# A fused RWKV and mixture-of-experts layer on one core: four PSUM places for the head's transposes, k weights loaded earlier, more products in the head

## The chip, the cores and the metric

The kernel runs on one core of one Trainium2 chip. The metric is the device time of one execution in microseconds; the time before is the median of three runs. A core has five engines that take their instructions in order, each from its own queue: TensorE (PE, matmuls; its weight loads are shown as PEld), VectorE (DVE), ScalarE (ACT), GpSimd (POOL) and SyncE (SP, which here only issues DMAs). Matmuls write to PSUM; all else lies in SBUF or in DRAM.

## What is computed

The input x has 2048 rows (tokens) of 512 float32 values. The reference normalises each row and adds to x the results of two branches that both read the normalised rows:

```python
xn = _layernorm(x, axis=-1)
# branch 1: RWKV attention; x is (1, 2048, 512): one sequence of 2048 tokens
r, v, k = jnp.split(einsum('btc,dc->btd', xn, W_rvk), 3, axis=-1)
def step(carry, kv):                  # p, q, o per channel
    no = maximum(o, u + kt);   A = exp(o - no);      Bc = exp(u + kt - no)
    y = (A * p + Bc * vt) / (A * q + Bc)
    no2 = maximum(w + o, kt);  A2 = exp(w + o - no2); B2 = exp(kt - no2)
    return (A2 * p + B2 * vt, A2 * q + B2, no2), y
attn = einsum('btc,dc->btd', sigmoid(r) * y, W_out)
# branch 2: 8 experts and 4 "zero" experts, the best 2 of 12 per token
probs = softmax(xn @ classifier_w.T)
_, idx = top_k(probs + bias, 2);  rw = take_along_axis(probs, idx) * 1.5
expert_out = (silu(xn @ gate.T) * (xn @ up.T)) @ down.T        # per expert, 256 wide
ffn = sum over chosen experts of rw * expert_out + xn * (weight of the chosen zero experts)
out = x + attn + ffn
```

The step over time runs in order over the tokens, per channel.

## The kernel before

**Sizes and units.** The 2048 rows are four blocks (b = 0 to 3) of 512 rows; each block is four tiles of 128 rows. The 512 channels are four groups (c) of 128. A *unit* is one (b, c): 512 tokens of 128 channels. `units` lists the 16 of them, b slowest. For each unit `project(b, c)` (L259) makes three products k, v and r, in this order, each a sum over four matmuls into one PSUM place `mm` (two of them), then a copy to SBUF by ACT (for r an Exp). `project` is a generator that yields after each matmul; a float32 matmul appears in the trace as two records. This document calls one such yield a *step*: a unit has 12, a product (or group) 4. `fill(n)` (L340) emits n steps of the generator `products`, which covers the first LEAD = 4 units.

**Order.** The order of the instructions is written out by hand (`manual_schedule`): each engine gets its instructions in the order in which the Python program emits them. There are three stretches.

1. *The head* (L347 to L356). SP first issues the loads in the order of L107 to L123: x block 0, the classifier `cls`, x block 1, the k weights (`load_w(2)`), x blocks 2 and 3, the v weights (`load_w(1)`), the r weights (`load_w(0)`), small vectors, `w_out`. A load of a block of x is four DMAs of 256 KB, a `load_w` is one DMA of 1 MB. Then, per block: `norm` (mean and variance on DVE, the root `sd` on ACT, some small DVE operations, then x normalised in place, two row tiles on DVE and two on ACT, and stored to DRAM as `xs`); `turn_block` (16 PE transposes, four into each PSUM place `pt` of pool `ps_tr`, each place copied by ACT to `xnT`); `logits` (PE into `lg`, also of `ps_tr`, copied by ACT to `lgs`) and `add_quarters` (PE into `pl`). The loop emits them in this order:

```python
norm(0)
turn_block(0)
for b in range(NTB):
    if b + 1 < NTB:
        norm(b + 1)
    logits(b)
    fill(1)
    if b + 1 < NTB:
        turn_block(b + 1)
    add_quarters(b)
```

2. *Routing* (L359 to L548). DVE chooses the best two of 12 for all tokens, PE counts and sorts them into 25 tiles of 128 (token, expert) pairs (`pc`, then two sums of 16 matmuls into `pi`, which wait for DVE's `tok`), and the results are the tile's tokens and weights. Steps of products are put between by `fill(9)`, `fill(14)`, `fill(7)`. Then come the first gathers and weights of experts, the first scan (unit 0), `fill(2)`, `fill(4)`, `fill(4)`, and what is left of the first four units.

3. *The loop* (L774 to L812). A table of planned times is filled and sorted: for each unit the scan's four stages (`scan`, L282: DVE scans, ACT Exps, the reciprocal; UNIT = 19 apart), the products of the other 12 units and eight output tiles of `attention` as 44 groups of four steps, and for each of the 25 tiles `first_half` (L669: loads for tile i + 2, the up and gate matmuls `pg`, tanh, gather for i + 3) and `second_half` (L685: `unite(i + 1)` makes `xgT`, `flip(i + 2)` starts a DMA transpose, `finish(i - 2)` makes the down product `po`, `yo` and a scatter that adds to `out`). The work is emitted in the order of the planned times; the times themselves are not used by the chip. Then the output tiles of blocks 2 and 3 follow, the last ones on rows read back from `out`.

**Buffers.** A pool with n buffers gives a tile one of n places per tag in turn, and a write into a place waits until the readers of its last content are done. `ps_tr`, `ps_gu`, `ps_o` and `ps_mm` have two PSUM places each; `ps_gu` (tag `gu`) is used by the experts' `pg` alone. `kvp` has four places for each of k, v and r. `ex_p` has two and `wk1` one.

Of the kernel before, what the change touches and what calls it, by code (L numbers as in the profile page):

```python
# [26 lines left out]
F32 = mybir.dt.float32  # L27
# [8 lines left out]
P = 128  # L36
T = 2048
C = 512
CC = C // P
# [20 lines left out]
def layer(ctx: ExitStack, tc: tile.TileContext, x, w_rvk, w_out, decay, first, cls, ebias, gu, down, out):  # L60
    nc = tc.nc

    def pool(name, bufs, **kw):
        return ctx.enter_context(tc.tile_pool(name=name, bufs=bufs, **kw))
# [8 lines left out]
    basep = pool("base", 4)  # L73
    rp = pool("route", 1)
    small = pool("small", 2)
    kvp = pool("kv", 4)
    wk = pool("wk", 2)
    ex_p = pool("exp", 2)
    dram = pool("dram", 1, space=bass.MemoryType.DRAM)
# [10 lines left out]
    def load_x(b):  # L90

        if b < 3:
            t = ewp.tile([P, NJ, C], F32, tag="gw", name=f"x{b}")
        else:
            t = xyp.tile([P, NJ, C], F32, tag="xy", name=f"x{b}")
        for j in range(NJ):
            i = b * NJ + j
            nc.sync.dma_start(t[:, j, :], x[i * P : (i + 1) * P, :])
            xt[i] = t[:, j, :]
# [3 lines left out]
    def load_w(n):  # L103
        wrvk_sb[n] = keep.tile([P, CC, C], F32, tag=f"wrvk{n}", name=f"wrvk{n}")
        nc.sync.dma_start(wrvk_sb[n], w_rvk[n])

    load_x(0)  # L107
    cls_sb = const.tile([P, CC, QW], F32, tag="cls", name="cls_sb")
    nc.sync.dma_start(cls_sb, cls)
    load_x(1)  # L110
    load_w(2)
    load_x(2)
    load_x(3)
    load_w(1)
# [80 lines left out]
    def norm(b):  # L195
        js = slice(b * NJ, (b + 1) * NJ)
        for j in range(NJ):
            i = b * NJ + j
            st = small.tile([P, 6], F32, tag="st", name=f"st{i}")
            nc.vector.bn_stats(st, xt[i])  # L200
            nc.vector.bn_aggr(mv[:, i, :], st)
        var = mv[:, js, 1]
        ve = small.tile([P, NJ], F32, tag="ve", name=f"ve{b}")
        nc.vector.tensor_scalar_add(ve, var, EPS)
        sd = small.tile([P, NJ], F32, tag="sd", name=f"sd{b}")
        nc.scalar.activation(sd, var, AF.Sqrt, bias=eps_sb[:, 0:1])
        r0 = small.tile([P, NJ], F32, tag="r0", name=f"r0{b}")
        nc.vector.reciprocal(r0, sd)

        sq = small.tile([P, NJ], F32, tag="sq", name=f"sq{b}")  # L210
        nc.vector.tensor_mul(sq, r0, r0)
        nc.vector.tensor_mul(sq, sq, ve)
        nc.vector.tensor_scalar(sq, sq, -0.5, 1.5, ALU.mult, ALU.add)
        nc.vector.tensor_mul(rstd[:, js], r0, sq)
        nc.vector.scalar_tensor_tensor(shift[:, js], mv[:, js, 0], -1.0, rstd[:, js], ALU.mult, ALU.mult)
        for j in range(NJ):
            i = b * NJ + j
            t, r = xt[i], rstd[:, i : i + 1]
            if j % 2 == 0:
                nc.vector.tensor_scalar(t, t, mv[:, i, 0:1], r, ALU.subtract, ALU.mult)  # L220
            else:
                nc.scalar.activation(t, t, AF.Identity, bias=shift[:, i : i + 1], scale=r)
        store_xn(b)

    def turn_block(b):
        xnT[b] = xyp.tile([P, CC, TB], F32, tag="xy", name=f"xnT{b}")
        for c in range(CC):
            pt = ps_tr.tile([P, TB], F32, tag="tr", name=f"pt{b}_{c}")
            for j in range(NJ):
                nc.tensor.transpose(pt[:, j * P : (j + 1) * P], xt[b * NJ + j][:, c * P : (c + 1) * P], ident)  # L230
            nc.scalar.copy(xnT[b][:, c, :], pt)
# [27 lines left out]
    def project(b, c):  # L259

        n = f"{b}_{c}"
        for name, m in (("k", 2), ("v", 1), ("r", 0)):
            ps = ps_mm.tile([P, TB], F32, tag="mm", name=f"p{name}{n}")
            for k in range(CC):
                nc.tensor.matmul(  # L265
                    ps,
                    wrvk_sb[m][:, k, c * P : (c + 1) * P],
                    xnT[b][:, k, :],
                    start=(k == 0),
                    stop=(k == CC - 1),  # L270
                )
                if k < CC - 1:
                    yield
            t = kvp.tile([P, TB], F32, tag=name, name=f"{name}{n}")
            if name == "r":
                nc.scalar.activation(t, ps, AF.Exp, scale=-1.0)
            else:
                nc.scalar.copy(t, ps)
            kvr[b, c, name] = t
            yield  # L280
# [50 lines left out]
        for _ in gen:  # L331
            pass

    def lead():
        for u in range(LEAD):
            yield from project(*units[u])

    products = lead()

    def fill(n):  # L340
        for _ in range(n):
            next(products, None)
# [6 lines left out]
    for b in range(NTB):  # L349
        if b + 1 < NTB:  # L350
            norm(b + 1)
        logits(b)
        fill(1)
        if b + 1 < NTB:
            turn_block(b + 1)
        add_quarters(b)  # L356
# [135 lines left out]
    NK = 2 * NT  # L492
    lowhot = xyp.tile([P, NK, P], BF16, tag="xy", name="lowhot")
    pi = ps_o.tile([P, NV, MAX_TILES], F32, tag="o", name="pi")
    fill(14)
    for m in range(2):
        ks = slice(m * NT, (m + 1) * NT)
        nc.vector.tensor_tensor(
# [83 lines left out]
    def turn(i):  # L582

        pt = ps_tr.tile([P, CC, P], F32, tag="tr", name=f"px{i}")
        for c in range(CC):
            nc.tensor.transpose(pt[:, c, :], st[i]["xg"][:, c * P : (c + 1) * P], ident)
        xgT = ex_p.tile([P, CC, P], F32, tag="xgT", name=f"xgT{i}")
        nc.scalar.copy(xgT, pt)
        st[i]["xgT"] = xgT

# [7 lines left out]

    def unite(i):

        xgT = ex_p.tile([P, CC, P], F32, tag="xgT", name=f"xgT{i}")
        nc.scalar.copy(  # L602
            xgT.bitcast(U16).rearrange("p c (t h) -> p c t h", h=2),
            st[i]["xq"].rearrange("p (h c) t -> p c t h", h=2),
        )
        st[i]["xgT"] = xgT
# [11 lines left out]
    def activate(i):  # L618
        pg = st[i]["pg"]

        th = ex_p.tile([P, INTER], F32, tag="th", name=f"th{i}")
        nc.scalar.activation(th, pg[:, 0, :], AF.Tanh, scale=0.5)  # L622
        nc.vector.scalar_tensor_tensor(th, th, 1.0, pg[:, 0, :], ALU.add, ALU.mult)  # L623
        act = ex_p.tile([P, INTER], F32, tag="act", name=f"act{i}")
        nc.vector.tensor_mul(act, th, pg[:, 1, :])
        st[i]["act"] = act

    def turn_act(i):
        pt = ps_tr.tile([P, IC, P], F32, tag="tr", name=f"pa{i}")
        for c in range(IC):  # L630
            nc.tensor.transpose(pt[:, c, :], st[i]["act"][:, c * P : (c + 1) * P], ident)
        actT = ex_p.tile([P, IC, P], F32, tag="actT", name=f"actT{i}")
        nc.scalar.copy(actT, pt)
        st[i]["actT"] = actT

# [6 lines left out]
        st[i]["aq"] = aq  # L642

    def unite_act(i):
        actT = ex_p.tile([P, IC, P], F32, tag="actT", name=f"actT{i}")
        nc.scalar.copy(
            actT.bitcast(U16).rearrange("p c (t h) -> p c t h", h=2),
            st[i]["aq"].rearrange("p (h c) t -> p c t h", h=2),
        )
        st[i]["actT"] = actT  # L650
# [105 lines left out]
    fill(2)  # L756
    stages = [scan(*u) for u in units]
    next(stages[0])
    next(stages[0])
    fill(4)  # L760
    next(stages[0])
    flip(0)
    flip(1)
    fill(4)
    next(stages[0])
    gather(2)
    fill(LEAD * 3 * CC)
    unite(0)


# [1 line left out]


    UNIT = 19.0  # L774
    ahead = [p for p in [project(*u) for u in units[LEAD:]] for _ in range(3)]
    after = {14: (0, 0), 15: (0, 1), 20: (0, 2), 21: (0, 3), 34: (1, 0), 35: (1, 1), 42: (1, 2), 43: (1, 3)}
    groups = len(ahead) + len(after)
    total = groups * 3.43 + TILES * 5.2
    table = []

    def plan(at, what, *args):
        table.append((at, iter([(what, *args)]) if args else what))

    for u in range(1, len(units)):
        for at in (0, 4, 6, 12):
            plan((u - 1) * UNIT + at, stages[u])
    one = total / groups / CC
    for m in range(groups):
        if m in after:
            b, j = after[m]  # L790
            group = attention(b, [j])
            plan(CC * m * one - 16, read_xn, b, [j])

            plan(CC * (m + 2 - j % 2) * one + 1, group)
        else:
            group = ahead.pop(0)
        for k in range(CC):
            plan((CC * m + k) * one, group)


    spread = (total - 14) / TILES
    for i in range(TILES):
        plan(6 + spread * i, first_half, i, TILES)
        plan(6 + spread * (i + 0.6), second_half, i, TILES)
    plan(8 + spread * (TILES - 1), read_xn, NTB - 2)
    plan(9 + spread * TILES, read_xn, NTB - 1)
    plan(6 + spread * TILES, turn_act, TILES - 1)
    plan(9 + spread * TILES, finish, TILES - 1)
    for _, work in sorted(table, key=lambda entry: entry[0]):
        todo = next(work, None)  # L810
        if todo:
# [73 lines left out]
```

## Time and profile before

| | |
|---|---|
| median of three runs | 392.39 us (392.27 to 393.36) |
| profiled execution, its own time | 392.65 us |
| its span in the trace | 390.9 us |
| TensorE busy | 374.4 us (96%) |
| VectorE busy | 270.7 us (69%) |
| ScalarE busy | 169.9 us (43%) |
| GpSimd busy | 97.3 us (25%) |
| first matmul starts at | 9.30 us |
| moved by DMA | 88.80 MB |

The span runs from the first instruction to the last. Busy times overlap between the engines. All instants in this document are from the start of the span. In a timeline row the columns are the start in us, the time from the first start to the last end of the merged instructions in us, engine, line, operation, what is written <- what is read, shape, and the number of instructions merged (x8); square brackets hold the idle time before them and what ended it. In the view of waits the columns after the colon are us in total, times, and the longest in us.

### The profile page before, as it was taken

To read this page: it belongs to the slowest core of one execution; us is meant where nothing else is said; L and a number is where in the kernel's file an instruction comes from. 1 tells how busy PE (TensorE), PEld (TensorE's weight loads), DVE (VectorE), ACT (ScalarE), POOL (GpSimd) and SP (SyncE) were. 2 spreads that over 40 slices of the span, in tenths; PEclk is the share of its full clock that TensorE was granted. 3 is DMA by queue.
4 is the path that set the end of the run, shared out by engine and by line. 5 is a ranking of instruction groups with operands and counts; after the bars stand their busy time and mean duration, and the time that the engine had idled before them with its cause. 6 is when DMAs were issued, how large, how long until landed. Compare 5 with 4: busy or idle time off the path is not lost. (4 is left out here: it accounts for less than half of the span.)

```text
span 390.9 us, 3494 instructions
## 1 busy us (share of the span) xinstructions
PE 374.4 (96%) x994; PEld 169.8 (43%) x994; DVE 270.7 (69%) x397; ACT 169.9 (43%) x278; POOL 97.3 (25%) x130
## 2 busy tenths in 40 slices
PE   0999999999999999999999999999999999999995
PEld 0545445444444444444444444444444444434442
DVE  5872898998965694859585769485948693938405
ACT  2675112534745455554364445555546355322000
POOL 5002001410223232213332133442223211412510
PEclk9999999999999999999999999999999999999999
DMA  8999908455698979998999998989998989673494
GB/s 264 408 346 387 323 29 322 114 156 162 155 292 197 299 175 206 321 239 204 248 299 245 245 249 145 304 222 273 227 292 215 275 157 242 160 233 51 56 197 151
DMA packets 62884, 88.80 MB, mean 227 GB/s; under 512 B 42192, under 2 KB 42320, under 8 KB 59088
## 3 DMA queue, kind: packets, MB, share of 16 engines
q1 hardware_dynamic: 55328, 67.85, 60.8%
q0 software_dynamic: 7536, 20.71, 24.3%
q8 instruction: 8, 0.13, 0.1%
q14 instruction: 12, 0.10, 0.1%
HBM read 63.78 MB, written 19.40 MB: 213 GB/s over the span
## 5 line engine op out<-in xcount | busy, mean ns | idle before, releaser
L614 PE MATMUL pg<-gw,xgT 128*128 128x512 f32 x200 | 90.1, 592 | 0.0
L660 POOL DMA_INDIRECT out_dram<-yo,to_i x25 | 44.7, 1789 | 156.7 <-ACT yo L659 75.9
L265 PE MATMUL pk<-xnT,wrvk 128*128 128x512 f32 x128 | 60.5, 596 | 0.0
L265 PE MATMUL pv<-xnT,wrvk 128*128 128x512 f32 x128 | 59.7, 593 | 0.0
L265 PE MATMUL pr<-xnT,wrvk 128*128 128x512 f32 x128 | 59.5, 592 | 0.0
L614 PEld LDWEIGHTS pg<-gw,xgT 128*128 128x128 f32 x200 | 37.8, 190 | 47.5 <-issue 46.2
L733 PE MATMUL pw<-wout_sb,yT 128*128 128x512 f32 x128 | 57.3, 593 | 0.1
L323 DVE RECIPROCAL den<-den 128x512 f32<-128x512 f32 x16 | 53.5, 3345 | 0.0
L623 DVE SCALAR_TENSOR_TENSOR th<-th,pg 128x256 f32<-128x256 f32 x25 | 10.5, 420 | 61.4 <-ACT th L622 61.4
L655 PE MATMUL po<-dw,actT 128*128 128x512 f32 x100 | 47.1, 593 | 0.8 <-ACT yo L659 0.8
L622 ACT ACTIVATE th<-pg 128x256 f32<-128x256 f32 x25 | 9.6, 384 | 68.4 <-PE pg L614 68.4
L556 POOL DMA_INDIRECT xg<-xs,token_i x25 | 26.8, 1072 | 48.8 <-DVE empty L543 27.5
L733 PEld LDWEIGHTS pw<-wout_sb,yT 128*128 128x128 f32 x128 | 24.2, 190 | 30.6 <-issue 30.4
L265 PEld LDWEIGHTS pk<-xnT,wrvk 128*128 128x128 f32 x128 | 23.8, 190 | 31.3 <-issue 30.6
L265 PEld LDWEIGHTS pv<-xnT,wrvk 128*128 128x128 f32 x128 | 24.2, 190 | 30.1 <-issue 29.2
L265 PEld LDWEIGHTS pr<-xnT,wrvk 128*128 128x128 f32 x128 | 24.2, 190 | 30.1 <-issue 29.7
L309 DVE TENSOR_TENSOR_SCAN sums<-obv,state,a 128x512 f32<-128x512 f32 x16 | 20.5, 1283 | 18.5 <-ACT obv L303 18.5
L655 PEld LDWEIGHTS po<-dw,actT 128*128 128x128 f32 x100 | 18.9, 190 | 25.0 <-issue 22.5
L602 ACT COPY xgT<-xq 128x1024 uint16<-128x1024 uint16 x25 | 28.9, 1158 | 0.0
L594 ACT COPY xp<-xg 128x1024 uint16<-128x1024 uint16 x25 | 26.1, 1046 | 4.4 <-DMA xq<-xp 3.3
L659 ACT ACTIVATE yo<-po,wplace 128x512 f32<-128x512 f32 x25 | 17.2, 686 | 24.2 <-PE po L655 24.2
L230 PE MATMUL pt<-ident,x 128*128 128x128 f32 x64 | 12.5, 326 | 11.0 <-DVE x L220 9.3
(153 smaller groups left out, 364.7 us busy)
## 6 DMA issues: line engine op xcount, KB each, us to landing
gw<-in_gu_dram SPq DMA_DIRECT2D x25, 1024.0 KB, 7.5
dw<-in_down_dram SPq DMA_DIRECT2D x25, 512.0 KB, 4.2
x<-in_x_dram SPq DMA_DIRECT2D x16, 256.0 KB, 5.4
xs<-x SPq DMA_DIRECT2D x16, 256.0 KB, 4.1
wrvk<-in_w_rvk_dram SPq DMA_DIRECT2D x3, 1024.0 KB, 7.4
xrow<-xs SPq DMA_DIRECT2D x8, 256.0 KB, 5.2
out_dram<-xrow POOLq DMA_DIRECT2D x8, 256.0 KB, 6.8
xrows<-xs SPq DMA_DIRECT2D x8, 256.0 KB, 6.9
```

Of the source, the lines that this page charges most:

```text
L230: nc.tensor.transpose(pt[:, j * P : (j + 1) * P], xt[b * NJ + j][:, c * P : (c + 1) * P], ident)
L265: nc.tensor.matmul(ps, wrvk_sb[m][:, k, c * P : (c + 1) * P], xnT[b][:, k, :], start=(k == 0), stop=(k == CC - 1),)
L309: nc.vector.tensor_tensor_scan(sq, bs, a2, s[:, 3:4], ALU.add, ALU.mult)
L323: nc.vector.reciprocal(den, den)
L556: nc.gpsimd.indirect_dma_start(out=xg, out_offset=None, in_=xs, in_offset=bass.IndirectOffsetOnAxis(ap=token[:, i : i + 1], axis=0),)
L594: nc.scalar.copy(xp, st[i]["xg"].bitcast(U16).rearrange("p (c h) -> p h c", h=2))
L602: nc.scalar.copy(xgT.bitcast(U16).rearrange("p c (t h) -> p c t h", h=2), st[i]["xq"].rearrange("p (h c) t -> p c t h", h=2),)
L614: nc.tensor.matmul(pg, st[i]["xgT"][:, c, :], st[i]["w"][:, c, :], start=(c == 0), stop=(c == CC - 1))
L655: nc.tensor.matmul(po, st[i]["actT"][:, c, :], st[i]["d"][:, c, :], start=(c == 0), stop=(c == IC - 1))
L659: nc.scalar.activation(yo, po, AF.Identity, scale=weight[:, i : i + 1])
L660: nc.gpsimd.indirect_dma_start(out=out, out_offset=bass.IndirectOffsetOnAxis(ap=to[:, i : i + 1], axis=0), in_=yo, in_offset=None, compute ...
L733: nc.tensor.matmul(po, yT[b][:, c, j * P : (j + 1) * P], wout_sb[:, c, :], start=(c == 0), stop=(c == CC - 1),)
```

## The change

Line numbers after the change are four to five higher. The change

- adds a fifth place for k and v (`kvp`) and a pool `er` of its own, with four places, for r;
- moves the DMA of the k weights ahead of `cls` and x block 1;
- lets the odd transposes of `turn_block` go to `ps_gu`'s two places, so that four are in use in turn;
- emits 5, 2, 2 and 2 steps of products in the four rounds of the head in place of 1 each, at two points of a round, and 15, 2, 3, 4, 5 later in place of 14, 2, 4, 4 and a rest; in all 56 steps precede the loop in place of 48, and the loop has 42 groups in place of 44;
- plans scans 7 earlier, experts 2 earlier and output tiles of attention two groups earlier in the loop's table;
- gives the experts' `xgT`, `th` and `actT` one place in place of two (`wk1`).

```diff
-    kvp = pool("kv", 4)
+    kvp = pool("kv", 5)
+    erp = pool("er", 4)
...
     load_x(0)
+    load_w(2)
     cls_sb = const.tile([P, CC, QW], F32, tag="cls", name="cls_sb")
     nc.sync.dma_start(cls_sb, cls)
     load_x(1)
-    load_w(2)
...
         for c in range(CC):
-            pt = ps_tr.tile([P, TB], F32, tag="tr", name=f"pt{b}_{c}")
+            if c % 2 == 0:
+                pt = ps_tr.tile([P, TB], F32, tag="tr", name=f"pt{b}_{c}")
+            else:
+                pt = ps_gu.tile([P, TB], F32, tag="gu", name=f"pt{b}_{c}")
...
-            t = kvp.tile([P, TB], F32, tag=name, name=f"{name}{n}")
+            t = (erp if name == "r" else kvp).tile([P, TB], F32, tag=name, name=f"{name}{n}")
...
-    def lead():
-        for u in range(LEAD):
+    def all_products():
+        for u in range(len(units)):
             yield from project(*units[u])
 
-    products = lead()
+    products = all_products()
...
             norm(b + 1)
+        fill(1 if b else 2)
         logits(b)
-        fill(1)
+        fill(1 if b else 3)
         if b + 1 < NTB:
             turn_block(b + 1)
...
-    fill(14)
+    fill(15)
...
-        xgT = ex_p.tile([P, CC, P], F32, tag="xgT", name=f"xgT{i}")
+        xgT = wk1.tile([P, CC, P], F32, tag="xgT", name=f"xgT{i}")
...
-        th = ex_p.tile([P, INTER], F32, tag="th", name=f"th{i}")
+        th = wk1.tile([P, INTER], F32, tag="th", name=f"th{i}")
...
-        actT = ex_p.tile([P, IC, P], F32, tag="actT", name=f"actT{i}")
+        actT = wk1.tile([P, IC, P], F32, tag="actT", name=f"actT{i}")
...
     next(stages[0])
+    fill(3)
     next(stages[0])
     fill(4)
...
-    fill(4)
+    fill(5)
     next(stages[0])
     gather(2)
-    fill(LEAD * 3 * CC)
     unite(0)
...
-    after = {14: (0, 0), 15: (0, 1), 20: (0, 2), 21: (0, 3), 34: (1, 0), 35: (1, 1), 42: (1, 2), 43: (1, 3)}
-    groups = len(ahead) + len(after)
+    after = {12: (0, 0), 13: (0, 1), 18: (0, 2), 19: (0, 3), 32: (1, 0), 33: (1, 1), 40: (1, 2), 41: (1, 3)}
+    groups = 3 * (len(units) - LEAD) - 2 + len(after)
...
-            plan((u - 1) * UNIT + at, stages[u])
+            plan((u - 1) * UNIT - 7 + at, stages[u])
...
-    spread = (total - 14) / TILES
+    spread = (total - 12) / TILES
     for i in range(TILES):
-        plan(6 + spread * i, first_half, i, TILES)
-        plan(6 + spread * (i + 0.6), second_half, i, TILES)
+        plan(4 + spread * i, first_half, i, TILES)
+        plan(4 + spread * (i + 0.6), second_half, i, TILES)
```

More of the change, by code (lines that the diff above doesn't have):

```diff
@@ L599, in unite @@
     def unite(i):
-        xgT = ex_p.tile([P, CC, P], F32, tag="xgT", name=f"xgT{i}")
+        xgT = wk1.tile([P, CC, P], F32, tag="xgT", name=f"xgT{i}")
         nc.scalar.copy(
@@ L631, in turn_act @@
             nc.tensor.transpose(pt[:, c, :], st[i]["act"][:, c * P : (c + 1) * P], ident)
-        actT = ex_p.tile([P, IC, P], F32, tag="actT", name=f"actT{i}")
+        actT = wk1.tile([P, IC, P], F32, tag="ap", name=f"actT{i}")
         nc.scalar.copy(actT, pt)
@@ L644, in unite_act @@
     def unite_act(i):
-        actT = ex_p.tile([P, IC, P], F32, tag="actT", name=f"actT{i}")
+        actT = wk1.tile([P, IC, P], F32, tag="actT", name=f"actT{i}")
         nc.scalar.copy(
@@ L763, in layer @@
     flip(1)
-    fill(4)
+    fill(5)
     next(stages[0])
     gather(2)
-    fill(LEAD * 3 * CC)
     unite(0)
     UNIT = 19.0
-    ahead = [p for p in [project(*u) for u in units[LEAD:]] for _ in range(3)]
-    after = {14: (0, 0), 15: (0, 1), 20: (0, 2), 21: (0, 3), 34: (1, 0), 35: (1, 1), 42: (1, 2), 43: (1, 3)}
-    groups = len(ahead) + len(after)
+    after = {12: (0, 0), 13: (0, 1), 18: (0, 2), 19: (0, 3), 32: (1, 0), 33: (1, 1), 40: (1, 2), 41: (1, 3)}
+    groups = 3 * (len(units) - LEAD) - 2 + len(after)
     total = groups * 3.43 + TILES * 5.2
@@ L795, in layer @@
         else:
-            group = ahead.pop(0)
+            group = products
         for k in range(CC):
             plan((CC * m + k) * one, group)
-    spread = (total - 14) / TILES
+    spread = (total - 12) / TILES
     for i in range(TILES):
-        plan(6 + spread * i, first_half, i, TILES)
-        plan(6 + spread * (i + 0.6), second_half, i, TILES)
[L805 to L808, printed above, removed]
+        plan(4 + spread * i, first_half, i, TILES)
+        plan(4 + spread * (i + 0.6), second_half, i, TILES)
+    plan(6 + spread * (TILES - 1), read_xn, NTB - 2)
+    plan(7 + spread * TILES, read_xn, NTB - 1)
+    plan(4 + spread * TILES, turn_act, TILES - 1)
+    plan(7 + spread * TILES, finish, TILES - 1)
     for _, work in sorted(table, key=lambda entry: entry[0]):
```

## Prediction

> **What bounds the kernel now.** First the page: busy time of each engine, and the slices of the span.
>
> ```profile
> PE 374.4 (96%) x994; PEld 169.8 (43%) x994; DVE 270.7 (69%) x397; ACT 169.9 (43%) x278; POOL 97.3 (25%) x130
> ...
> PE   0999999999999999999999999999999999999995
> ```
>
> TensorE is the bound: only the first slice and the last are not full. The change does not alter its work, so only idle time can be gained. The waits of PE, the second view, seem to leave little:
>
> ```profile
> PE pt L230 <- DVE x L220: 9.3, 1, 9.3
> PE pt L230 <- ACT x L222: 0.8, 3, 0.3
> PE po L655 <- ACT yo L659: 0.8, 1, 0.8
> PE pi L520 <- DVE tok L512: 0.6, 1, 0.6
> ```
>
> But ends of matmuls are modelled, so short stalls hide in "busy". The third view, PE's timeline, gives them by starts:
>
> ```profile
> 9.30 4.13 PE L230 MATMUL pt<-ident,x 128*128 128x128 f32 x16 [9.30 <-DVE x L220]
> ...
> 21.23 1.12 PE L265 MATMUL pk<-xnT,wrvk 128*128 128x512 f32 x2
> 22.20 0.68 PE L230 MATMUL pt<-ident,x 128*128 128x128 f32 x3
> 23.14 2.46 PE L230 MATMUL pt<-ident,x 128*128 128x128 f32 x13 [0.27 <-ACT x L222]
> 25.43 0.96 PE L252 MATMUL pl<-quarters,lgs 128*128 128x12 f32 x8
> 26.32 1.07 PE L239 MATMUL lg<-xnT,cls_sb 128*32 128x512 f32 x8
> 27.32 1.13 PE L265 MATMUL pk<-xnT,wrvk 128*128 128x512 f32 x2
> ```
>
> A head block takes 27.32 - 21.23 = 6.09 us. Its work, by distances between starts: one step of a product (two records) 0.86, the logits 1.0, add_quarters 0.89, and 16 transposes at 0.11 = 1.76; together 4.5. So 1.6 us of each block is lost, though hardly any is shown as idle. What sets the 6.09 is on ACT and DVE:
>
> ```profile
> 22.99 0.57 ACT L248 COPY lgs<-lg 128x512 f32<-128x512 f32 x1
> ...
> 24.30 1.12 ACT L231 COPY xnT<-pt 128x512 f32<-128x512 f32 x2 [0.21 <-PE pt L230]
> 25.63 0.59 ACT L231 COPY xnT<-pt 128x512 f32<-128x512 f32 x1 [0.21 <-PE pt L230]
> 26.12 0.30 ACT L206 ACTIVATE sd<-mv,eps_sb 128x4 f32<-128x4 f32 x1
> ```
>
> ```profile
> 25.68 0.17 DVE L204 TENSOR_SCALAR ve<-mv 128x4 f32<-128x4 f32 x1
> ...
> 26.45 0.18 DVE L208 RECIPROCAL r<-sd 128x4 f32<-128x4 f32 x1 [0.60 <-ACT sd L206]
> ```
>
> It is a ring: the root sd of the next block stands in ACT's queue behind this block's four copies out of PSUM; those wait for transposes, which wait for copies because pt has two places (the 0.21 twice). DVE waits 0.60 for sd.
>
> **The change, part by part.** All instants are of the profiled execution.
>
> *Four PSUM places.* Copies of xnT then follow at ACT's own pitch (two in a row, 0.535), so the fourth starts 1.6 us after the first, against 2.13 (23.50 to 25.63). The ring becomes: sd, 1.53 later ACT's two x, 1.43 later lgs, then the copies. DVE has a floor too: from sd to its next mv complete is 5.65 (20.03 to 25.68). So a block could take 5.65 rather than 6.09. That by itself is a gain only because PE gets work to fill it.
>
> *More products in the head.* 5, 2, 2 and 2 steps in the four rounds, 11 in place of 4: seven steps of 0.859 = 6.01 us of PE work leave the stretch behind the head. The gain is 6.01 less the delay of the head's end, 35.18 now.
>
> *The k weights moved ahead of cls and x's second block.* SP issues one DMA earlier than five others, which land later by its megabyte (about 2.6 us at the pace of x's landings, 256 KB each 0.67). cls is needed at 13.35 and landed at 6.4: free. x's second block was complete at 9.9 and will be at about 12.4, where the k weights landed before; its statistics end at about 13.3. sd of this block starts at 13.94 in either kernel, behind block 0's copies, so this costs 0, with 0.6 us to spare; were that cover gone, up to 0.6. Steps 1 to 4 of the first product find their weights by about 9 to 10.
>
> *The fifth step.* It is the first one of v, and stands in PE's queue ahead of block 1's transposes. Its weights are in the second weights DMA, issued at 13.1 and unmoved: the same bytes go before it.
>
> ```profile
> L105 SPq DMA_DIRECT2D wrvk<-in_w_rvk_dram x1: 328/328/328, 13.1 to 13.1; - x1
> ...
> DMA to landing us min/median/max: 7.2/7.2/7.2
> ```
>
> So it lands at 20.3. PE gets there at about 18.1: transposes of block 0 to 13.2 (their pitch of 0.213 leaves the four places nothing to save), two steps to 15.4, logits to 16.4, two steps. PE idles 2.2, and the transposes, x's copies and the next root wait behind it:
>
> - step 5 starts at 20.33, block 1's transposes at 21.3 (now 16.25), copies from 21.98, sd of block 2 at 24.05 (now 20.03);
> - sd of block 3 at DVE's floor, 24.05 + 5.65 = 29.7 (now 26.12); PE's 5.4 of work a block (4.5 + 0.86) fits beside;
> - from there ACT: x to 32.65, the copy of v (new here, 0.53), lgs, xnT from 33.7 to 35.9. PE: transposes stopped for lgs's place to 33.8, done at 34.7; then add_quarters, step, logits, step, add_quarters: 0.89 + 0.86 + 1.0 + 0.86 + 0.89, to 39.15.
>
> The head ends 3.97 later with 6.01 more done: gain 2.04.
>
> *Behind the head.* 45 steps and 3 in the table up to the first pg, against 44 and 4: equal. The one more ahead of the first pi fills the idle there:
>
> ```profile
> 56.47 1.55 PE L520 MATMUL pi<-tok,lowhot 128*128 128x200 bf16 x16 [0.58 <-DVE tok L512]
> ```
>
> The last pk ahead starts at 55.30, so 56.47 is 0.74 late; tok follows the head's end by the same DVE chain. The second pi was 0.15 late, of which 0.1 goes. Gain 0.84.
>
> *Single buffers in the experts* (xgT, th, actT). Writing xgT(i+1) must wait for the pg matmuls of i; but it stands on ACT behind tanh(i), which waits for those anyway. th is read by DVE within some us, and the next tanh comes 11 later; actT(i)'s reader, po, stands on PE ahead of the next tile's pg, whose tanh is ahead of the next actT on ACT. Cost 0; were the cover of xgT gone, a copy of 1.16 and its wait would lie in each tile. The other places (k, v five, r apart four) let the two groups run ahead that leave the table; k of a unit reuses a place whose scan is planned 20 or more earlier.
>
> *The table.* Scans come 7 earlier, attention two groups and experts 2 earlier, and 6.0 us of products leave a loop that has no idle now:
>
> ```profile
> 81.00:387.00 306.00, 304.92 (x713) 134.32 (x711) 207.77 (x249) 137.04 (x222) 83.89 (x69) 1.00 0.88 216
> ```
>
> Tile to tile, pg is 11 us apart and becomes 0.24 closer. The experts' weights land 9 us or more ahead of their pg, by the timelines. The tight place is early:
>
> ```profile
> 98.55 1.14 ACT L602 COPY xgT<-xq 128x1024 uint16<-128x1024 uint16 x1
> ```
>
> xgT(2) ends at 99.69, and its pg starts at 99.78. In the new order the root of the trouble, ACT's Exp pair of the scan, stands ahead of it with a copy of v, and PE comes with one step less between tiles 0 and 1. By ACT's order I get 98.25 for xgT against 98.0 for pg, in instants of the tok chain: 0.3 lost (between 0 and 1.2, one copy). POOL's scatters and SP's loads keep their order to the tail; the tail's chain on POOL (scatters one after another, then rows of out read back at 377.6) keeps the same PE work behind it: 0.
>
> **Sum:** 6.01 - 3.97 + 0.84 - 0.3 = 2.6. The profiled execution took 392.65 (span 390.9, 1.75 around it), 0.26 over the median 392.39. After: span 388.3, itself 390.05; against the median, 389.8.
>
> **A rule against it.** The first row of PE's timeline has 16 transposes at 0.21 apart, the later ones stand at 0.11: after the idle start the array ran at half pace until about 14. The Trainium skill ("TensorE: Matmul & The Clock Gate", "What's actually happening") puts the fall to half clock at an idle window of about 3.4 us, in windows that run freely. The new idle of 2.2 us is shorter, so I charge nothing; no row of this trace has an idle of that length in mid-run. Were the gate to close, one window at half pace loses at most 1.7.
>
> **The rivals.**
>
> - *The v weights do not hold PE* (landing earlier, or reached late). Transposes of block 1 start at 19.0, sd of block 2 falls at 21.8, and the head ends at 36.75: 6.01 - 1.57 + 0.84 - 0.3 = 5.0, time 387.4. Against: 13.1 + 7.2, with the whole queue ahead of it unchanged in bytes. For: PE's way there is an estimate, and landings may shift by some tenths.
> - *The clock falls* in that wait: 389.8 + 1.7 = 391.5.
> - *The expert loop does not give the 6.0 us back.* Place: ACT's queue, where Exp pairs that wait for DVE now come a third of a scan earlier than the copies of xgT. PE would wait at pg, tile after tile. All 6.0 kept: the first pg is 3.13 later (3.97 - 0.84), so 395.5. It makes the kernel slower from about 4 us of new PE waits in the loop (2.9 gained without them, and 1.2 for what can be measured). For: the 0.1 us above. Against: in the other tiles xgT ends 0.6 to 5.5 us ahead of pg (timelines of ACT and PE), and ACT is busy for 137 of 306 us.
>
> **How the numbers follow.** A measurement here can tell about 0.3%, 1.2 us. The forecast has 0.56 (0.51 of it faster by more), the first rival 0.22, the clock 0.12 (half of it within the bound), the loop 0.10 (0.06 slower). Faster 0.79, same 0.14, slower 0.07. The range goes from the first rival with the lower ends of the costs, 387.2, to just past the clock's case, 391.9.
>
> **What would show it.** Right: PE idle for about 2 us in front of a pv at 20.3, released by the weights' DMA; block 1's transposes at 21.3; ACT's sd at 24, then 29.7; the product behind the last pl at 39.2 (35.18 now); no idle at the first pi; span 388.3. Wrong: no gap at the first pv and a head that ends at 37 (the first rival); records of 0.86 apart after 20.3 (the clock); waits of PE on xgT that add up to 2 us or more in the loop.

## The result and the profile after

The changed kernel takes 389.76 us (median of four runs, 389.49 to 390.12), the kernel before beside it 392.61: ratio 0.9925 (95% interval 0.9907 to 0.9944), 2.85 us less. The forecast was 389.8. The profiled execution took 389.55, its span is 387.7 in place of 390.9: 3.2 us less. In two of the kernels below (with one step per head block, 9 of 13 runs; with extra transposes, 3 of 5) some runs had a mean granted clock of 0.995 or 0.996 in place of 0.998 to 1.000, for a reason that is open, and took 1.7 to 1.8 us longer than the others by their medians, about 0.4 to 0.5% of the span.

The page first: busy time of each engine in the changed kernel.

```profile
span 387.7 us, 3521 instructions
...
PE 372.0 (96%) x994; PEld 169.7 (44%) x994; DVE 270.6 (70%) x397; ACT 169.8 (44%) x278; POOL 94.4 (24%) x130
```

TensorE is as full as before. To see where 3.2 us came from, the span is cut in three at events that both kernels have: the first product behind the last pl (end of the head), and the first pg. This is the view by windows, before and then after. The columns are: stretch, its length, busy us and instructions of PE, PEld, DVE, ACT and POOL, granted clock, DMA share, GB/s.

```profile
0.00:35.18 35.18, 24.23 (x137) 13.90 (x137) 20.78 (x68) 20.11 (x36) 4.89 (x50) 1.00 0.94 346
35.18:80.89 45.71, 45.13 (x148) 21.49 (x148) 41.49 (x81) 12.69 (x21) 8.57 (x11) 1.00 0.64 214
80.89:391.00 310.11, 305.03 (x713) 134.43 (x711) 208.46 (x249) 137.04 (x222) 83.89 (x69) 1.00 0.87 215
```

```profile
0.00:38.88 38.88, 28.14 (x151) 16.47 (x151) 20.88 (x68) 21.07 (x37) 4.89 (x50) 1.00 0.87 326
38.88:83.74 44.86, 44.86 (x149) 21.49 (x149) 40.67 (x81) 12.21 (x22) 8.58 (x11) 1.00 0.60 201
83.74:388.00 304.26, 299.01 (x699) 131.75 (x697) 209.03 (x249) 136.56 (x220) 80.96 (x69) 1.00 0.87 220
```

The head grew by 3.70 us and took in 14 records (seven steps, 6.01 us of PE). The routing stretch became 0.85 shorter. The last stretch, to the true ends of the spans, went from 310.0 to 304.0, just the 6.0 us of products that left it. Together 3.70 - 0.85 - 6.01 = -3.16. The loop gave back all of its products' time; the whole gain is time in which PE stood, shown as idle or hidden between starts, ahead of the first pg.

PE's waits in the changed kernel:

```profile
PE pt L234 <- DVE x L221: 9.4, 1, 9.4
PE pv L269 <- DMA wrvk<-in_w_rvk_dram: 1.1, 1, 1.1
PE po L660 <- ACT yo L664: 0.8, 1, 0.8
PE pt L234 <- ACT lgs L252: 0.2, 1, 0.2
```

The forecast wait is in the second row: the first pv waits for its weights. The wait for tok is gone. PE's timeline in the head:

```profile
9.45 4.04 PE L234 MATMUL pt<-ident,x 128*128 128x128 f32 x16 [9.45 <-DVE x L221]
13.28 2.73 PE L269 MATMUL pk<-xnT,wrvk 128*128 128x512 f32 x4
15.94 1.07 PE L243 MATMUL lg<-xnT,cls_sb 128*32 128x512 f32 x8
16.93 1.98 PE L269 MATMUL pk<-xnT,wrvk 128*128 128x512 f32 x4
20.02 1.12 PE L269 MATMUL pv<-xnT,wrvk 128*128 128x512 f32 x2 [1.10 <-DMA wrvk<-in_w_rvk_dram]
20.98 1.91 PE L234 MATMUL pt<-ident,x 128*128 128x128 f32 x16
...
25.57 1.13 PE L269 MATMUL pv<-xnT,wrvk 128*128 128x512 f32 x2
26.53 1.91 PE L234 MATMUL pt<-ident,x 128*128 128x128 f32 x16
...
31.12 1.12 PE L269 MATMUL pr<-xnT,wrvk 128*128 128x512 f32 x2
```

In blocks 1 and 2 sixteen transposes now stand in one row of 1.91 us, with no break: four places are enough there. (Block 3 keeps one break of 0.18, for the place of lgs, which the forecast had.) A block takes 31.12 - 25.57 = 5.55 us with one step more in it, where it took 6.09. These 5.55 are PE's own work, row behind row. ACT and DVE are hardly faster:

```profile
27.17 2.05 ACT L235 COPY xnT<-pt 128x512 f32<-128x512 f32 x4
29.27 0.30 ACT L207 ACTIVATE sd<-mv,eps_sb 128x4 f32<-128x4 f32 x1
```

```profile
29.21 0.17 DVE L205 TENSOR_SCALAR ve<-mv 128x4 f32<-128x4 f32 x1
29.60 0.18 DVE L209 RECIPROCAL r<-sd 128x4 f32<-128x4 f32 x1 [0.22 <-ACT sd L207]
```

Four copies follow each other on ACT, and the root sd meets DVE's mv within 0.1. From the root before (23.53) it is 5.74, DVE's own round. So the ring of PE, places and copies is gone, and what is left is PE's work, 5.55, and DVE's floor, 5.74.

### The profile page after: what moved, and what is told of

Its sections match the earlier page's. It is cut to its first block, busy times and chain, and to the rows that moved or that the text cites. A ratio compares the mean times of both kernels' runs of the same rounds, so it can differ in the third digit from the quotient of the medians.

```text
span 387.7 us, 3521 instructions
## 1 busy us (share of the span) xinstructions
PE 372.0 (96%) x994; PEld 169.7 (44%) x994; DVE 270.6 (70%) x397; ACT 169.8 (44%) x278; POOL 94.4 (24%) x130
## 3 DMA queue, kind: packets, MB, share of 16 engines
q0 software_dynamic: 7536, 20.71, 24.4%
## 5 line engine op out<-in xcount | busy, mean ns | idle before, releaser
L665 POOL DMA_INDIRECT out_dram<-yo,to_i x25 | 41.5, 1661 | 156.1 <-ACT yo L664 88.1
L269 PE MATMUL pv<-xnT,wrvk 128*128 128x512 f32 x128 | 60.9, 595 | 1.1 <-DMA wrvk<-in_w_rvk_dram 1.1
L313 DVE TENSOR_TENSOR_SCAN sums<-obv,state,a 128x512 f32<-128x512 f32 x16 | 20.5, 1282 | 17.3 <-ACT obv L307 17.3
L315 DVE TENSOR_TENSOR_SCAN sums<-obv,state,a 128x512 f32<-128x512 f32 x16 | 20.6, 1286 | 0.6
```

The lines of the kernel that those rows point to most:

```text
L269: nc.tensor.matmul(ps, wrvk_sb[m][:, k, c * P : (c + 1) * P], xnT[b][:, k, :], start=(k == 0), stop=(k == CC - 1),)
L313: nc.vector.tensor_tensor_scan(sq, bs, a2, s[:, 3:4], ALU.add, ALU.mult)
L315: nc.vector.tensor_tensor_scan(sp, bvs, a2, s[:, 4:5], ALU.add, ALU.mult)
L665: nc.gpsimd.indirect_dma_start(out=out, out_offset=bass.IndirectOffsetOnAxis(ap=to[:, i : i + 1], axis=0), in_=yo, in_offset=None, compute ...
```

## The experiments

Times are medians against the kernel before on the same chip; for the changed kernel 389.76, and 389.34 in a second measurement. Intervals are 95%.

**The v weights ahead of x's block 3.**

```diff
-    load_x(3)
     load_w(1)
+    load_x(3)
```

> The changed kernel with the v weights' DMA ahead of x's block 3. Forecast's theory (the fifth step of the head holds block 1's transposes until the v weights land at 20.0): the weights land at about 17.5, step 5 starts at 18.9 in place of 20.02, the idle of 1.1 us in front of the first pv is gone, everything behind comes 1.1 to 1.2 us earlier, 388.6 us. Block 3 of x lands by 20.2, its statistics start after 22: no new wait. Rival (DVE's ring of the norm paces the head, the PE wait is slack in it): the head's end stays at 38.9, 389.8 us.

Measured: 387.90 us, ratio 0.9873 (0.9851 to 0.9895). All five runs (387.58 to 388.86) lie below all eight of the changed kernel (388.93 to 390.16). PE's timeline:

```profile
18.80 1.02 PE L269 MATMUL pv<-xnT,wrvk 128*128 128x512 f32 x2
19.66 1.91 PE L234 MATMUL pt<-ident,x 128*128 128x128 f32 x16
...
37.56 1.10 PE L269 MATMUL pr<-xnT,wrvk 128*128 128x512 f32 x2
```

No idle stands in front of the first pv, block 1's transposes start at 19.66 in place of 20.98, and the last row, the product behind the last pl, at 37.56 in place of 38.88: 1.32 earlier in both places (0.22 of it because PE's first transpose came at 9.23 in place of 9.45). What PE waits there is therefore on the path to the end, not slack of the norm's ring.

**The k weights behind x's block 1 again.**

```diff
     load_x(0)
-    load_w(2)
...
     load_x(1)
+    load_w(2)
```

> The changed kernel with the k weights' DMA back behind x's block 1. Forecast's theory: the weights land at 12.4, the first step starts at 13.3 behind the transposes anyway, and the root of block 1 stands behind block 0's copies in either order: 389.8 us, 0 within 0.3. Rival (the two steps in front of the logits need the earlier load): PE waits at the first pk, 0.5 to 1 us slower.

Measured: 389.53 us, ratio 0.9911 (0.9891 to 0.9930), not told apart from the changed kernel. Its first pk starts at 13.64, right behind block 0's transposes as in the changed kernel. The moved load is worth nothing that can be measured here.

**All transposes in two places.**

```diff
-            if c % 2 == 0:
-                pt = ps_tr.tile(...)
-            else:
-                pt = ps_gu.tile(...)
+            pt = ps_tr.tile(...)
```

> The changed kernel with all transposes in the two places of ps_tr. Forecast's theory: the third and fourth group of transposes wait for copies again, 0.5 us per block in three blocks, 391.2 us, and idle of PE before pt comes back. Rival (with products between, ACT and not the places paces the copies): below 0.3 us, 389.8.

Measured: 391.12 us, ratio 0.9954 (0.9944 to 0.9964): 1.4 to 1.8 more than the changed kernel. The breaks are back in PE's timeline, between the second and the third group of four:

```profile
20.60 1.04 PE L234 MATMUL pt<-ident,x 128*128 128x128 f32 x8
21.88 1.15 PE L234 MATMUL pt<-ident,x 128*128 128x128 f32 x8 [0.24 <-ACT xnT L235]
```

A block takes 31.78 - 25.70 = 6.08 us there. From the first transposes to the end of the head it is 30.90 us against 29.43: 1.47; from the first pv, 20.48 (40.12 - 19.64) against 18.86: 1.62, the 0.5 in each of three blocks that was forecast.

**One step per head block, the seven others in the loop.**

```diff
-        fill(1 if b else 2)
         logits(b)
-        fill(1 if b else 3)
+        fill(1)
...
-    groups = 3 * (len(units) - LEAD) - 2 + len(after)
+    groups = 3 * (len(units) - LEAD) + len(after)
```

(`after` has its old keys.)

> The changed kernel with one step of products per head block as before; the seven steps are done in the loop, which has its 44 groups again. Forecast's theory: the four places alone take a block from 6.09 to 5.65 us, the head ends at about 33.8 (35.2 before), and with the step ahead of pi the whole is 390.8 us: the extra steps in the head are worth 1.0. Rival (the head's gain is all in the extra steps, the ring keeps its 6.09): the head ends at 35.2, 391.8 us.

Measured: 394.38 us (392.50 to 395.75), ratio 1.0036 (1.0019 to 1.0052), a miss of 3.6 us. By its four runs at the full clock (median 392.96; the profiled one, 392.50, is among them) the miss is 2.2. In the trace the head did what the theory said: the head ends at 33.42, and sd to sd is 5.71, with ACT waiting for DVE, whose round is therefore the floor:

```profile
19.38 0.30 ACT L207 ACTIVATE sd<-mv,eps_sb 128x4 f32<-128x4 f32 x1 [0.18 <-DVE mv L202]
25.09 0.30 ACT L207 ACTIVATE sd<-mv,eps_sb 128x4 f32<-128x4 f32 x1 [0.18 <-DVE mv L202]
```

But then:

```profile
PE pg L618 <- ACT xgT L606: 2.3, 1, 2.3
```

The first pg waits for xgT(0). That chain (routing on DVE, gather, two flips, DMA transpose, unite) ended 47.2 us behind the head's end, in the changed kernel 44.2. ACT shows where; here, and then in the changed kernel:

```profile
71.58 0.59 ACT L282 COPY v<-pv 128x512 f32<-128x512 f32 x1 [1.80 <-PE pv L269]
72.06 1.05 ACT L598 COPY xp<-xg 128x1024 uint16<-128x1024 uint16 x1
77.97 1.05 ACT L598 COPY xp<-xg 128x1024 uint16<-128x1024 uint16 x1 [4.87 <-DMA xq<-xp]
```

```profile
74.94 1.04 ACT L599 COPY xp<-xg 128x1024 uint16<-128x1024 uint16 x1
79.47 1.05 ACT L599 COPY xp<-xg 128x1024 uint16<-128x1024 uint16 x1 [3.50 <-DMA xq<-xp]
```

The first flip (the copy to xp) starts 38.6 us behind the head's end in place of 36.1. The gathers were issued 31.5 us behind it in both kernels, so routing is not what is late: the flip stands in ACT's queue behind the copy of v, which waits 1.80 us for the product that PE has only just finished. The second flip then could not start before the first one's DMA transpose had landed, and ACT stood 4.87 us for that in place of 3.50 (why this transpose took longer is open). The copy of r, state and xgT(0) stood behind it.

**The same seven steps ahead of the first pg.**

```diff
-    fill(5)
+    fill(12)
```

(With one step per head block and the loop of the changed kernel.)

> One step per head block, and the seven steps put behind the second pi, ahead of the first pg, in place of the loop. Shown by the run with one step: the head ends at 33.4, and the first pg waited 2.3 us for xgT(0), whose chain took 47 us from the head's end. Theory (the extra steps are worth about 0.9 in the head; the rest of that run's loss was missing cover ahead of the first pg): no wait at the first pg, span 388.3, 390.2 us. Rival (steps are worth their full 6 us only in the head, wherever else they are put PE waits): 392 or more.

Measured: 392.19 us, ratio 0.9976 (0.9967 to 0.9984). Forecast 390.2: missed again. The first pg does not wait, but a product does:

```profile
80.28 3.70 PE L269 MATMUL pv<-xnT,wrvk 128*128 128x512 f32 x8 [1.16 <-ACT r L280]
```

It is the same place on ACT: the copy of r frees the product's PSUM place, and stands behind the flip that waits for the DMA transpose. From the first transposes to the head's end these two kernels take 24.31 and 24.63 us, the changed one 29.43 with 6.01 us of steps more. So the extra steps themselves saved about 0.9 to 1.2 in the head, as expected. The kernel before takes 25.88 there (35.18 - 9.30), so the four places save 1.3 to 1.6 in the head without the extra steps too; it is behind the head that this was lost again. What they are worth in all is more, because without them the same work lands where ACT is blocked; these two runs bound that only for their own two placements.

**Fourteen steps ahead of the first pi.**

```diff
-    fill(15)
+    fill(14)
...
-    fill(5)
+    fill(6)
```

> The changed kernel with 14 steps ahead of the first pi as before, the fifteenth put ahead of the first pg. Forecast's theory: PE waits for tok again, 0.75 us slower, 390.5. Rival (the step is only moved, tok's chain moves with it): 389.8.

Measured: 390.70 us (389.35 to 393.38), ratio 0.9940 (0.9922 to 0.9957). The wait for tok is back, but smaller, 0.41 us by starts (0.25 of it shown as idle):

```profile
60.53 1.55 PE L525 MATMUL pi<-tok,lowhot 128*128 128x200 bf16 x16 [0.25 <-DVE tok L517]
```

In the same trace the first pv waited 2.7 us for its weights, so the median is no measure of the one step. Counted from the start of the first pv, the trace is 0.5 us longer than the changed kernel's (see the last experiment): the direction is as expected, the size less than the 0.75 forecast.

**The scans where they were.**

```diff
-            plan((u - 1) * UNIT - 7 + at, stages[u])
+            plan((u - 1) * UNIT + at, stages[u])
```

> The changed kernel with the scans planned where they were (7 later). Forecast's theory: PE has no wait in the loop in either case, 389.8 within 0.3. Rival (products now run two groups ahead, so k, v and r places are freed too late without the shift and ACT's copies hold PE): idle of PE before products in the loop, 1 us or more slower.

Measured: 390.10 us, ratio 0.9924 (0.9906 to 0.9942): no difference, and no wait of PE in the loop but that of po. The shift of the scans does nothing that can be measured.

**xgT in two places, k and v in four.**

```diff
-    kvp = pool("kv", 5)
+    kvp = pool("kv", 4)
...
-        xgT = wk1.tile(...)
+        xgT = ex_p.tile(...)
```

> The changed kernel with xgT in two places again and k and v in four. Forecast's theory: the single place of xgT costs nothing, so two gain nothing; the fifth place of k and v is not waited for either, 389.8 within 0.3. Rivals: if the single place holds ACT, up to 1 us faster; if the fifth place is needed, PE waits at the first pg, 1 us slower or more.

Measured: 389.53 us, ratio 0.9905 (0.9886 to 0.9925): no difference. PE's four waits are those of the changed kernel, only the first pv's is longer (1.8). Both parts were taken back in one kernel, so the median alone could hide two effects that cancel; no wait on PE points to either.

**The changed kernel again, and two steps further.** The second kernel adds to the kernel with the v weights ahead:

```diff
+    warm = ps_mm.tile([P, TB], F32, tag="mm", name="warm")
+    for _ in range(36):
+        nc.tensor.transpose(warm[:, 0:P], ident, ident)
     norm(0)
```

and the third to that one:

```diff
-        if i == n - 1:
-            finish(i - 1)
...
+    plan(4 + spread * (TILES - 0.15), finish, TILES - 2)
     plan(4 + spread * TILES, turn_act, TILES - 1)
```

> The changed kernel once more, beside the next two on the same chip: 389.8 us. The wait of PE in front of the first pv follows the landing of the v weights, which differed between profiles (idle 0.6 to 2.7 us before that pv in kernels with the same head); so it should differ again here, within that.

> The kernel with the v weights ahead of x's block 3, and 36 more transposes of the identity into a PSUM place of the products ahead of the head, while PE has nothing to do (they compute nothing that is used). Theory (the array runs at half pace after the idle start, whatever it does first, and transposes count as activity): block 0's transposes come 0.11 apart in place of 0.21 and the first two steps at full pace, so that PE reaches step 5 about 2.5 us earlier, of which the wait for the v weights at about 17.4 takes back up to 1: 1.4 to 2.4 us less than 387.9, 385.5 to 386.5. Rival (transposes do not count as activity, the Trainium skill's statement): no change, 387.9. Second rival (block 0's copies on ACT and x's block 1 pace the start): below 0.7 us.

> The kernel of the run before, with the down product of tile 23 planned one step of attention behind that of tile 22, where both stood next to each other. Theory (the second waited 0.94 us for ACT to read the first one's place): that wait goes, 0.8 us less than the run before. Rival (POOL's scatters at the tail set the end): no change.

The changed kernel: 389.34 us (388.93 to 390.16), ratio 0.9910 (0.9894 to 0.9925). The wait in front of its first pv is 2.2 in this profile, against 1.1, though the time is the same within the spread of single runs:

```profile
PE pv L269 <- DMA wrvk<-in_w_rvk_dram: 2.2, 1, 2.2
```

In the profiled executions with this head and this load order it was 0.6, 1.1, 1.8, 2.2 and 2.7 us (the 0.6 stands under DVE's name in its list, but the weight load of the same step waits for the DMA). The weights explain only the smaller part of this. The first pv started at 20.02 to 20.71, always 7.1 to 7.5 us behind the issue of its weights' DMA, which SP reached at 12.9 to 13.6. PE, though, was ready for it at 18.0 to 20.0: its first transpose came at 9.45 to 10.38, and the array left half pace 3.6 to 5.9 us after that. In this profile it did so before the first product, whose four records start within 1.81 us (15.56 - 13.75) in place of 2.66:

```profile
10.02 3.89 PE L234 MATMUL pt<-ident,x 128*128 128x128 f32 x16 [10.02 <-DVE x L221]
13.75 1.88 PE L269 MATMUL pk<-xnT,wrvk 128*128 128x512 f32 x4
15.56 1.07 PE L243 MATMUL lg<-xnT,cls_sb 128*32 128x512 f32 x8
```

So an early PE only waits longer, and the start of the first pv sets all that follows. The span less that start is 367.6 to 367.7 us in both profiles of the changed kernel and in those with the k weights late, the v weights ahead, the scans or the places back, and the extra transposes below. It is 368.2 with 14 steps ahead of pi (0.5 more), 369.3 with two places (1.6 more) and 366.6 with the tail spread (1.0 less). This measures each of these three without the chance of the landing.

With the transposes ahead, PE's timeline of the start reads:

```profile
1.98 6.89 PE L353 MATMUL warm<-ident 128*128 128x128 f32 x36 [1.98 <-POOL ident masks.py:199]
9.30 0.83 PE L234 MATMUL pt<-ident,x 128*128 128x128 f32 x3 [0.43 <-DVE x L221]
10.39 1.64 PE L234 MATMUL pt<-ident,x 128*128 128x128 f32 x13 [0.26 <-ACT x L223]
11.87 1.88 PE L269 MATMUL pk<-xnT,wrvk 128*128 128x512 f32 x4
```

Block 0's transposes follow at 0.11, the first two steps take 1.81 us (13.68 - 11.87) in place of 2.93 in the kernel that it adds to, and the first pv starts at 16.90 in place of 18.80: 1.9 earlier, the span 384.6 in place of 386.4. The median is 388.13, though (386.42 to 388.48): three of its runs are among those at the lower clock, the other two took 386.42 and 386.57. The transposes are not what lowers it, since the next kernel has them too, at 0.998 or more in all five runs. By its trace and two runs this kernel is faster than the one with the v weights ahead; its median does not show it.

With the tail spread: 386.27 us (385.22 to 386.51), ratio 0.9829 (0.9815 to 0.9842), 3.1 less than the changed kernel beside it. The wait of po is gone from its list of waits:

```profile
PE warm L353 <- POOL ident masks.py:199: 2.0, 1, 2.0
PE pv L269 <- DMA wrvk<-in_w_rvk_dram: 1.3, 1, 1.3
PE pt L234 <- DVE x L221: 0.6, 1, 0.6
PE pt L234 <- ACT x L223: 0.3, 1, 0.3
```

Its profiled span, 384.7, is that of the run before, since its first pv started at 18.08 in place of 16.90. The difference of the two medians mixes the tail with the runs at the lower clock. The tail's worth is read from the trace: the wait is gone, and behind the first pv it is 366.6 us in place of 367.7, about 1.0 less where 0.8 was forecast.

## Why the prediction was right, point by point

- **The sum.** Forecast: the head's end 3.97 later with 6.01 us more done, 0.84 behind it, 0.3 lost in the loop: 2.6. Measured: 3.70, 6.01, 0.85 and 0: 3.16 of span. The medians differ by 2.85 (2.63 from the 392.39 that the forecast was made against). The mechanism and the gain were right; that 389.8 met 389.76 to the last digit is luck. Two terms were off by 0.3 each, and the start of the first pv alone moves by 0.7 from profile to profile.
- **The fifth step holds block 1's transposes.** Right, and the run with the v weights ahead shows that it is on the path. Its start was forecast at 20.33 and lay between 20.02 and 20.71. Its size was off in the first profile: idle 2.2 forecast, 1.1 measured, 0.6 to 2.7 in all five. Two terms of it: the first two steps took 2.66 us, not 2.2, because the array stayed at half pace to 14.99 (two records 0.85 apart), and the weights were there at 20.0, not 20.3. The first does not move the end, since PE would have waited; the second is about the 0.27 by which the head's end came early.
- **Four places take a block to DVE's floor.** 5.65 forecast, 5.74 and, with one step per block, 5.71 measured from sd to sd; two places give 6.08 from pv to pv again. What they are worth was not given a number of its own; it is 1.4 to 1.8 of the 2.9 by the medians, 1.6 by the traces. "A gain only because PE gets work to fill it" holds for the end, not for the head: there they save 1.3 to 1.6 without the work as well.
- **The k weights cost 0.** Right, and they also gain 0: like the shift of the scans and the places of k, v and xgT, it does nothing that can be measured here.
- **Single buffers, k and v places, scans: 0.** Right in both runs that tried it, the places as a pair. Not tried alone: the single places of th and actT, the separate pool for r, and the new places of experts and attention in the table.
- **The step ahead of pi.** In the changed kernel the idle is gone and the routing stretch is 0.85 shorter (0.84 forecast); taking the step away brought back a wait of 0.41 in one trace and 0.5 behind the first pv.
- **0.3 lost at the third tile.** Wrong by its whole size. xgT(2) again ends 0.1 us before its pg (100.50 + 1.16 against 101.76), by the rows of ACT and PE in the changed kernel:

```profile
100.50 1.16 ACT L607 COPY xgT<-xq 128x1024 uint16<-128x1024 uint16 x1
```

```profile
101.76 3.66 PE L619 MATMUL pg<-gw,xgT 128*128 128x512 f32 x8
```

- **"45 and 3 against 44 and 4: equal".** Right for this change, but it was treated as a matter of counting. The two runs with one step per head block have the count or more, and take 2.4 (47.29 - 44.86) and 1.4 (52.30 - 6.01 - 44.86) us more than the changed kernel from the head's end to the first pg, for the same work: what must fit is the place of the copies on ACT beside the flips, not the number of steps on PE.
- **The rivals.** The first one's mechanism is what the run with the v weights ahead made true, and its price, 387.4, was near the 387.9 measured. The clock did not fall: behind idle of 1.1 to 2.7 us the transposes still came 0.11 apart. No idle of PE in mid-run was longer than 2.7, so the rule that the forecast cited is not tested. The price of 1.7 that it put on one window may be too low: at the start of ten of the profiles half pace lasted 3.6 to 6.1 us, a loss of 1.8 to 3 us (an estimate from these figures). The loop gave back all of the 6.0 us.

## What to carry to other kernels

When steps are moved forward into idle time of an in-order engine, look up for each of them when its operand lands: one step whose weights were late held up everything queued behind it, and a change in the order of the loads was worth 1.3 us more in the trace. A ring of engines that runs through a queue (here a root behind four copies behind two places) shows hardly any idle in a list of waits; distances between starts of the same instruction in successive rounds show it. And cover that a moved piece of work gives at its old place has to be counted before it is moved: here the same steps, put elsewhere, met ACT's queue at a worse place: a flip stood behind a copy that waited for PE, and other copies stood behind a flip that waited for a DMA transpose. Last, when a wait depends on a landing that shifts from run to run, compare traces from the instant at which the wait ends: effects of 0.5 to 1.6 us could be told apart in that way.

## What the hardware showed beyond that

Transposes alone bring the array to full pace. In the kernel with 36 extra transposes PE did nothing else before 9.30 us. This is the view by windows, with the columns as above:

```profile
2.00:7.50 5.50, 5.50 (x26) 5.50 (x27) 3.44 (x9) 0.45 (x3) 3.48 (x41) 1.00 0.95 357
7.60:8.70 1.10, 1.10 (x11) 1.02 (x9) 0.91 (x6) 0.00 (x0) 0.00 (x0) 1.00 1.03 389
```

The first 26 filled 5.5 us, 0.213 apart by their starts, and the last ones came 0.109 apart (one that spans the cut is counted in both rows); the pace changed at about 7.6, 5.6 us after the first. The Trainium skill ("TensorE: Matmul & The Clock Gate", "Part 4: PE-mode transpose") says that the full clock does not engage for transposes, because they do not count as a busy PE in the same way; for these float32 transposes the measurement decides. The time to full pace is no constant: over ten profiles it was 3.6 to 6.1 us from PE's first instruction. The granted clock in the profile's rows is 1.00 all that time, so the pace at the start is read from distances between starts alone.
